# Turning normalized tokens into channels on VectorE in 32x32 blocks where no convolution runs

## The chip, the core and the metric

The kernel runs on one core of a Trainium2 chip. A core has five engines that work side by side, each through its own queue in order: TensorE (PE, matrix multiplication, with its weight loads shown apart as PEld), VectorE (DVE), ScalarE (ACT), GpSimd (POOL) and SyncE (SP), which here only issues DMA transfers. TensorE writes to PSUM, a small memory of eight banks; everything else lives in SBUF, with 128 partitions. The metric is device microseconds for one execution, fewer being better.

## The reference

The input is a batch of 2 images of 56 x 56 tokens with 384 channels, in fp32. Layer 0 is neighborhood attention with 12 heads of 32 channels over a 7 x 7 window, and a feed-forward network (MLP). Layer 1 is a depthwise 3 x 3 convolution with four scans over rows and columns, and a second MLP. Each step adds its input to its output.

```python
# layer 0
h = neighborhood_attention(layer_norm(x, ln1_g, ln1_b), w_qkv, b_qkv, rpb, w_proj, b_proj)
x = x + h
y = layer_norm(x, ln2_g, ln2_b)
x = x + gelu(y @ w1 + b1) @ w2 + b2
# layer 1
p = _layernorm(x, n1_g, n1_b) @ w_in + b_in
local = conv3x3_depthwise(p, k_conv)
mixed = 0.25 * (ema(local, left) + ema(local, right) + ema(local, down) + ema(local, up)) + local
x = x + _layernorm(mixed, on_g, on_b) @ w_out + b_out
h2 = _layernorm(x, n2_g, n2_b)
x = x + gelu(h2 @ w1 + b1) @ w2 + b2
```

Every layer norm works on a token's 384 (or 768) channels, and every product contracts over channels.

## The kernel before

The kernel computes in fp32 throughout. The work falls into three stages.

**Attention** runs over 14 groups of 448 tokens (8 rows of an image), each cut into 4 windows of 8 x 14 queries, each window into 3 units of 4 heads. One step `s` of the loop at L702 is one unit; there are 168. A unit's scores (L515) go to two PSUM banks, `biased` (L530, DVE) adds the bias, `numerators` (L536, ACT) takes the exponential into `pts`. The keys of a window lie in `m` chunks, two at the images' edges and three inside. `gathered` (L538) adds the chunks up on VectorE into `sum`, one step later. `values` (L546), two steps later, multiplies `pts` by the values `vt`, chunk by chunk, and then `sum` by ones (L558), which gives the denominators. Between these, TensorE computes queries, keys and values of later groups and projects finished tiles of 128 tokens (`project`, L573). In the last two groups (`n >= END`) there is nothing left to prepare beyond the last group's own queries, and projections come at the fixed steps in `THEN`. A projected tile is added to its residual `xr` (L585) after GpSimd has added a bias to `xr` (L571), either some steps after its load (`loaded`, a countdown from 4, L797) or just before the addition. The store of the tile is issued by `store_all` at the start of the next step, and right behind it the load of the residual of the tile three further on, into the buffer that the store reads (`bufs=3`). SP's queue is in order: these loads, the windows' `vt` (L465), the biases (L316) and, from step 152 on, the first MLP's six weight parts of 0.8 MB (L620) stand behind one another. At s == NU (L736) the keys' memory is given back, and the four last residuals and the first two groups of the attention's output (`xs`) are loaded. After the loop come the last projections, and the norm of `xs[0]` (L810). The PSUM banks of attention are then given back to the next stage, which needs their last readers, the additions at L585, to be done.

**The first pass** (L1341) runs over 13 groups of 2, 3 and then eleven times 4 tiles of 128 tokens. For a group `g` it computes twelve pieces of the hidden layer (`hidden`, L1053: a product from channels `hT`, then Gelu on ACT), and then the group's tokens, one tile at a time (`tokens`, L1059), in two PSUM banks called `y`. Beside this it takes the group before (`gw`, called `waiting`) on to layer 1: ACT normalizes it during hidden steps 2 to 5, `channels_n1` makes it into channels at step 11, and `project_in` multiplies by `w_in` and stores to `p_d`. The next group's norm (ln2) is taken during steps 3 to 10, and its `channels` stand after `project_in`, ahead of the tokens.

`channels` (L1038) calls `to_channels` (L245): for each of 3 channel blocks TensorE transposes each 128x128 piece (L251) into a PSUM bank, and ACT takes the bank to `hT` with the norm's gain and bias (L254).

**The convolution** runs on VectorE beside the two passes. A planner, `Beside` (L113), holds a list of jobs (`Band`, `Columns`), written out as small steps with an estimated cost. Each call `beside.go(worth)` in the passes lets out as many steps as are due. Jobs are added by `project_in` once enough image rows are there, for the first time while g is 3. `beside.busy()` tells whether any are left.

**The last pass** (L1428) runs over groups of eleven times 4, 3 and 2 tiles. The mixed tokens of a group are loaded by `load_mix` (L1233) two groups ahead as 6 channel blocks `mx`. Their norm's statistics are needed by token, so `measure` (L1246) transposes six 128x128 pieces per tile on TensorE (L1251) into PSUM, where VectorE reads them; `measure_beside` spreads the tiles over the hidden steps of the group before. `project_out` (L1266) multiplies by `w_out`. Then come the tokens of the group, and between its last two tiles the `channels` (n2) of the next. Group 6 is called `half_way`: its tokens reach into the second image, so the planner must be run to its end (`beside.until`) before `load_mix(6)`, at the end of g=4. For this group alone `measure_beside` starts two steps later (`late=2`).

Of the kernel before, what the change touches and what calls it, by code (L numbers as in the profile page):

```python
# [33 lines left out]
F32 = mybir.dt.float32  # L34
# [7 lines left out]
NH, KS, HD = 12, 7, 32  # L42
# [131 lines left out]
def block_kernel(ctx: ExitStack, tc: tile.TileContext, ins: dict, out: bass.AP):  # L174
# [328 lines left out]
    class Unit:  # L503
# [34 lines left out]
        def gathered(self):  # L538

            n, t = self.w.keys, lp.tile([P, 4, TT], F32, name="sum", bufs=2)  # L540
            self.sum = t
            nc.vector.tensor_tensor(t[:n], self.pts[:n, :, 0, :], self.pts[:n, :, 1, :], ALU.add)
            for c in range(2, self.m):
                nc.vector.tensor_tensor(t[:n], t[:n], self.pts[:n, :, c, :], ALU.add)

        def values(self):  # L546

            w, hg, n = self.w, self.hg, self.w.keys
            for c in range(self.m):
                for i in range(4):  # L550
                    h = 4 * hg + i
                    nc.tensor.matmul(
                        o[i * HD : (i + 1) * HD, hg, :],
                        lhsT=w.vt[:n, c, h * HD : (h + 1) * HD], rhs=self.pts[:n, i, c, :],
                        start=c == 0, stop=c == self.m - 1,
                    )
            for i in range(4):
                nc.tensor.matmul(  # L558
                    sums[i * HD : (i + 1) * HD, hg * TT : (hg + 1) * TT], lhsT=ones_hd[:n, :],
                    rhs=self.sum[:n, i, :], start=True, stop=True,  # L560
                )

    def load_residual(t, pool=lp, bufs=3):

        xrs[t] = pool.tile([P, C], F32, name="xr", bufs=bufs)
        nc.sync.dma_start(out=xrs[t], in_=xf[t * P : (t + 1) * P, :])
        loaded[t] = 4
# [134 lines left out]
    for s in range(NU + 4):  # L702
        n, k, hg, i = s // UG, s % UG, s % NC, s // NC
        store_all()
# [31 lines left out]
        if s == NU:  # L736
            kctx.close()
            xp = ctx.enter_context(tc.tile_pool(name="x", bufs=2, side="right", reuse_waits="tile"))
            tail_pool = actx.enter_context(tc.tile_pool(name="a_tail", bufs=1))
            for t in range(T2 // P - 4, T2 // P):  # L740
                load_residual(t, tail_pool, 4)
            xs = {g: load_group(x1f, groups[g], "xa") for g in range(2)}

# [63 lines left out]

    for take in taking:
        take()
    norm = norm_of(xs[0], groups[0][1], sm)  # L810
    norm.close(groups[0][1])
# [148 lines left out]
    def passes(xs, xn, w1, w2, between=lambda psum: None):  # L960
# [81 lines left out]

        def columns(w, m, hT, n):

            ps = ps_m.tile([P, MT], F32, name="mm")
            for c in range(NC):
                nc.tensor.matmul(  # L1047
                    ps[:, : n * P], lhsT=w[:, c, m * P : (m + 1) * P], rhs=hT[:, c, : n * P],
                    start=c == 0, stop=c == NC - 1,
                )  # L1050
            return ps
# [181 lines left out]
        def load_mix(g):  # L1233
            t0, n = dgroups[g]
            mx = io.tile([P, NI, MT], F32, name="mx")
            for b, at, here, n in images(t0, n * P):
                nc.sync.dma_start(
                    out=mx[:, :, here : here + n],
                    in_=mix_d[b][:, :, at : at + n].rearrange("m p t -> p m t"),
                )  # L1240
# [16 lines left out]
        def measure_beside(m, g, ahead, late=0):  # L1257

            n = dgroups[g][1]
            k = (m - late) // 2 - 1  # L1260
            if m % 2 == 1 and 0 <= k < n:
                measure(ahead[0], ahead[2], k)
            if m == min(10 + late, NHID - 1):
                ahead[2].close(n)
# [73 lines left out]
        def channels_n1(xn, n):  # L1338
            return channels(xn, n, "L1_conv_n1_g", "L1_conv_n1_b")

        for g, (t0, n) in enumerate(groups):  # L1341
            hid = []
            preparing = prepare_w_out() if g == 1 else iter(())
# [4 lines left out]
            for m in range(NHID):  # L1348
                next(preparing, None)
                if waiting is not None:  # L1350
# [5 lines left out]
                    if 2 <= m < 2 + groups[gw][1]:  # L1356
                        norm_w.apply_by_scalar(m - 2, x2w, xn_w)
                    if m == (11 if g == 1 else 6):
                        store_x2(gw, x2w)
                    if m == NHID - 1:  # L1360
                        hT_w = channels_n1(xn_w, groups[gw][1])
# [27 lines left out]
            if g < last:  # L1389
                hT = channels(xn_next, n_next, "L0_conv_ln2_g", "L0_conv_ln2_b")  # L1390
# [23 lines left out]
        hT = channels_n1(xn, groups[g][1])  # L1414
# [12 lines left out]
        hT = channels(first["xn"], dgroups[0][1], "L1_conv_n2_g", "L1_conv_n2_b")  # L1427
        for g, (t0, n) in enumerate(dgroups):  # L1428
            hid = []
            for m in range(NHID):  # L1430
                hid.append(hidden(w1, m, hT, n, "L1_conv_b1"))
                if g < last:
                    measure_beside(m, g + 1, ahead, 2 if g + 1 == half_way else 0)
# [6 lines left out]
            for k in range(n):  # L1440
                if k == n - 1 and g < last:
                    hT = channels(xn, dgroups[g + 1][1], "L1_conv_n2_g", "L1_conv_n2_b")
                ps = tokens(hid, w2, k)
                o = res[:, k, :]
                if k == 0 and g < last:
                    norm.shift(dgroups[g + 1][1])
                nc.vector.tensor_tensor(o, ps, o, ALU.add)  # L1447
                nc.sync.dma_start(out=yout[t0 + k * P : t0 + (k + 1) * P, :], in_=o)
                if k == n - 3 and g < last:
                    xn = normalized(norm, x3, dgroups[g + 1][1])  # L1450
# [95 lines left out]
```

## Time and profile before

| | us |
|---|---|
| median of 3 runs | 2710.99 (2710.21 to 2712.02) |
| the profiled execution, its own time | 2709.48 |
| its span, first to last instruction | 2707.7 |

The main groups of instructions of the profile, by line, as far as the change touches them or their neighbours (busy time is that of the group taken together, so pipelined instructions count once):

| line, engine | what | count | busy us | mean ns |
|---|---|---|---|---|
| L1063 PE | tokens, `y<-w,hid` | 2352 | 764.8 | 486 |
| L1047 PE | hidden, `mm<-hT,w` | 1872 | 776.1 | 570 |
| L251 PE | transposes of `channels`, 128x128 | 441 | 55.4 | 275 |
| L1251 PE | transposes of `measure`, 128x128 | 294 | 40.8 | 276 |
| L254 ACT | `hT<-tp`, 128x512 form | 99 | 69.7 | 776 |
| L482, L498 DVE | block transposes in attention, 128x352 | 56 + 56 | 30.5 + 30.0 | 544, 536 |
| L558 PE | sums, in all its forms | 1344 | 63.1 | 259 to 261 |
| L1141 DVE | taps of the convolution | 336 | 377.1 | 1122 |

How to read the profile: each engine has a row of 40 slices, and a digit is its busy share in tenths. Durations of matmuls are from start to modelled end and overlap, so what one costs in a stream is the distance between starts. A wait is named after the engine and line that released it. One fp32 matmul appears as two instructions, one transpose as one. The granted clock (PEclk) is TensorE's clock as a share of full speed.

### The profile page before, as it was taken

To read this page: it belongs to the slowest core of one execution; us is meant where nothing else is said; L and a number is where in the kernel's file an instruction comes from. 1 tells how busy PE (TensorE), PEld (TensorE's weight loads), DVE (VectorE), ACT (ScalarE), POOL (GpSimd) and SP (SyncE) were. 2 spreads that over 40 slices of the span, in tenths; PEclk is the share of its full clock that TensorE was granted. 3 is DMA by queue.
4 is the path that set the end of the run, shared out by engine and by line. 5 is a ranking of instruction groups with operands and counts; after the bars stand their busy time and mean duration, and the time that the engine had idled before them with its cause. 6 is when DMAs were issued, how large, how long until landed. Compare 5 with 4: busy or idle time off the path is not lost. (4 is left out here: it accounts for less than half of the span.)

```text
span 2707.7 us, 36333 instructions
## 1 busy us (share of the span) xinstructions
PE 2659.7 (98%) x14975; PEld 1492.9 (55%) x14975; DVE 1679.7 (62%) x2560; ACT 897.7 (33%) x1447; POOL 249.6 (9%) x264
## 2 busy tenths in 40 slices
PE   8999999998899999999999999999999999999998
PEld 4666666655555555555554555555555455555565
DVE  3778877878320188688989888898888522221110
ACT  4555555554222332222344422321233211111111
POOL 1111111111211100000010000000100011110100
PEclk9999999999999999999999999999999999999999
DMA  6423454225410132232354544443354411011000
GB/s 213 133 88 104 150 174 149 77 75 167 135 47 27 64 115 79 104 118 98 120 199 183 206 143 141 164 136 117 142 188 171 153 47 44 12 41 35 30 12 16
DMA packets 131887, 298.91 MB, mean 110 GB/s; under 512 B 10646, under 2 KB 87552, under 8 KB 129408
## 3 DMA queue, kind: packets, MB, share of 16 engines
q1 hardware_dynamic: 131712, 296.50, 31.9%
q8 instruction: 119, 1.95, 0.3%
q14 instruction: 56, 0.46, 0.1%
HBM read 180.86 MB, written 115.61 MB: 109 GB/s over the span
## 5 line engine op out<-in xcount | busy, mean ns | idle before, releaser
L1047 PE MATMUL mm<-hT,w 128*128 128x512 f32 (+2 forms) x1872 | 776.1, 570 | 0.1
L1063 PE MATMUL y<-w,hid 128*128 128x384 f32 x2352 | 764.8, 486 | 0.0
L1063 PEld LDWEIGHTS y<-w,hid 128*128 128x128 f32 x2352 | 445.0, 190 | 305.3 <-issue 0.5
L1047 PEld LDWEIGHTS mm<-hT,w 128*128 128x128 f32 x1872 | 352.1, 191 | 372.8 <-issue 342.4
L1056 ACT ACTIVATE hid<-mm,chan 128x512 f32<-128x512 f32 (+2 forms) x312 | 206.3, 662 | 741.2 <-PE mm L1047 741.2
L1141 DVE SCALAR_TENSOR_TENSOR loc<-pt,taps,loc 128x990 f32<-128x990 f32 (+9 forms) x336 | 377.1, 1122 | 10.0 <-ACT loc L1123 1.7
L536 ACT ACTIVATE pts<-pts 119x448 f32<-119x448 f32 (+3 forms) x336 | 206.5, 642 | 187.9 <-DVE pts L530 187.9
L530 DVE TENSOR_TENSOR pts<-sc,bias 119x448 f32<-119x448 f32 (+3 forms) x336 | 220.8, 699 | 67.7 <-PE sc L515 66.7
L222 POOL TENSOR_TENSOR rs<-rs,mhalf 128x4 f32<-128x4 f32 (+4 forms) x67 | 87.2, 1302 | 1745.6 <-DVE rs L219 1704.1
L386 PE MATMUL ps<-hT,wqkv 128*128 128x448 f32 x504 | 211.9, 559 | 3.5 <-ACT vs L431 1.5
L1047 PE MATMUL mm<-hT,w_in 128*128 128x512 f32 (+2 forms) x468 | 191.7, 568 | 0.6 <-ACT hT L254 0.6
L1063 PE MATMUL y<-w_out,mx 128*128 128x384 f32 x588 | 191.8, 486 | 0.0
L1395 DVE TENSOR_TENSOR xc<-y,xa 128x384 f32<-128x384 f32 x49 | 27.3, 557 | 251.0 <-PE y L1063 250.5
L1447 DVE TENSOR_TENSOR xc<-y,xc 128x384 f32<-128x384 f32 x49 | 27.2, 555 | 218.2 <-PE y L1063 167.8
L1063 PEld LDWEIGHTS y<-w_out,mx 128*128 128x128 f32 x588 | 111.6, 190 | 79.8 <-issue 4.8
L240 ACT ACTIVATE xn<-xc,sh,rs 128x384 f32<-128x384 f32 x98 | 64.7, 698 | 269.3 <-DVE sh L233 269.1
L214 DVE BATCH_NORM_STATS2 st<-xi 128x6 f32<-128x384 f32 x98 | 50.3, 554 | 153.3 <-PE xi L1251 153.2
L1047 PEld LDWEIGHTS mm<-hT,w_in 128*128 128x128 f32 x468 | 88.7, 190 | 101.6 <-issue 91.8
L386 PEld LDWEIGHTS ps<-hT,wqkv 128*128 128x128 f32 x504 | 90.2, 191 | 84.4 <-issue 72.8
L254 ACT ACTIVATE hT<-tp,chan 128x512 f32<-128x512 f32 (+2 forms) x117 | 79.5, 751 | 165.1 <-PE tp L251 165.0
L515 PEld LDWEIGHTS sc<-qT,kT 32*100 32x100 f32 (+3 forms) x3168 | 90.9, 169 | 69.5 <-DVE pts L530 17.3
L515 PE MATMUL sc<-qT,kT 32*100 32x112 f32 (+3 forms) x3168 | 113.8, 270 | 9.0 <-DVE pts L530 8.4
(89 smaller groups left out, 2435.4 us busy)
## 6 DMA issues: line engine op xcount, KB each, us to landing
bias<-in_bias_t SPq DMA_DIRECT2D x16, 1344.0 KB
loc<-loc_d SPq DMA_DIRECT2D x24, 784.0 KB
mixed<-mix_d SPq DMA_DIRECT2D x24, 784.0 KB
mix_d<-mixed SPq DMA_DIRECT2D x24, 784.0 KB
xa<-x_d SPq DMA_DIRECT2D x22, 768.0 KB
p_d<-mx SPq DMA_DIRECT2D x10, 1536.0 KB
mx<-mix_d SPq DMA_DIRECT2D x10, 1536.0 KB
pt<-p_d SPq DMA_DIRECT2D x18, 560.0 KB
```

The costliest lines, as they stand in the source:

```text
L214: nc.vector.bn_stats(st[:n, i, :], x)
L222: nc.gpsimd.tensor_tensor(rs, rs, mhalf[:n, :k], ALU.pow)
L240: nc.scalar.activation(out[:, k, :], x[:, k, :], AF.Identity, bias=self.sh[:n, k : k + 1], scale=self.rs[:n, k : k + 1],)
L254: nc.scalar.activation(dst[:, c, : len(xs) * n], tp, AF.Identity, bias=col(b, c), scale=col(g, c))
L386: nc.tensor.matmul(ps, lhsT=wqkv[:, c, m * P : (m + 1) * P], rhs=hT[:, c, half_of(n)], start=c == 0, stop=c == NC - 1,)
L515: nc.tensor.matmul(sc[i // 2][: w.keys, i % 2, (first + c) * TT : (first + c + 1) * TT], lhsT=kT[d, hg, w.keys_at + r * w.kc : w.keys_at + ...
L530: nc.vector.tensor_tensor(self.of(half), sc[half][:n, :, at].rearrange("p h (c q) -> p h c q", q=TT), self.w.bias[:n, 4 * self.hg + h : 4 ...
L536: nc.scalar.activation(self.of(half), self.of(half), AF.Exp)
L1047: nc.tensor.matmul(ps[:, : n * P], lhsT=w[:, c, m * P : (m + 1) * P], rhs=hT[:, c, : n * P], start=c == 0, stop=c == NC - 1,)
L1056: nc.scalar.activation(t[:, : n * P], ps[:, : n * P], AF.Gelu, bias=col(b1, m))
L1063: nc.tensor.matmul(ps, lhsT=t[:, k * P : (k + 1) * P], rhs=w[:, m, :], start=m == 0, stop=m == len(lhs) - 1,)
L1141: nc.vector.scalar_tensor_tensor(to, pt[:, lo + dy - self.top : hi + dy - self.top, xt : xt + n], self.tap(dy, dx), to, ALU.mult, ALU.add,)
```

## The change

Where no convolution runs, the transposition of normalized tokens into channels goes from TensorE to VectorE. This engine turns 32x32 blocks; so a 128x128 piece is turned by 16 instructions, one for each pair of 32-partition strips, each over all channel blocks at once. In both passes the flag `by_vector` decides, and in the last pass `measure_by_vector` replaces `measure` for the groups after half way. Three other parts go with it: in attention's last two groups the denominators are summed over the chunks by TensorE instead of VectorE; the loads at s == NU move to the start of the step, with `xs` ahead of the residuals, and the norm of `xs[0]` ahead of the takes; the load of the half-way group is cut by tiles, and its `late` goes.

```diff
         def gathered(self):
-            n, t = self.w.keys, lp.tile([P, 4, TT], F32, name="sum", bufs=2)
-            self.sum = t
+            n, self.parts = self.w.keys, [self.pts[:, :, c, :] for c in range(self.m)]
+            if self.w.n >= END:
+                return
+            t = lp.tile([P, 4, TT], F32, name="sum", bufs=2)
+            self.parts = [t]
...
-            for i in range(4):
-                nc.tensor.matmul(
-                    sums[i * HD : (i + 1) * HD, hg * TT : (hg + 1) * TT], lhsT=ones_hd[:n, :],
-                    rhs=self.sum[:n, i, :], start=True, stop=True,
-                )
+            for c, part in enumerate(self.parts):
+                for i in range(4):
+                    nc.tensor.matmul(
+                        sums[i * HD : (i + 1) * HD, hg * TT : (hg + 1) * TT], lhsT=ones_hd[:n, :],
+                        rhs=part[:n, i, :], start=c == 0, stop=c == len(self.parts) - 1,
+                    )
...
-        loaded[t] = 4
+        loaded[t] = steps
...
     for s in range(NU + 4):
         n, k, hg, i = s // UG, s % UG, s % NC, s // NC
+        if s == NU:
+            kctx.close()
+            xp = ctx.enter_context(tc.tile_pool(name="x", bufs=2, side="right", reuse_waits="tile"))
+            tail_pool = actx.enter_context(tc.tile_pool(name="a_tail", bufs=1))
+            xs = {g: load_group(x1f, groups[g], "xa") for g in range(2)}
+            for t in range(T2 // P - 4, T2 // P):
+                load_residual(t, tail_pool, 4, 2)
         store_all()
...
-        if s == NU:
-            kctx.close()
...
-            for t in range(T2 // P - 4, T2 // P):
-                load_residual(t, tail_pool, 4)
-            xs = {g: load_group(x1f, groups[g], "xa") for g in range(2)}
...
+    norm = norm_of(xs[0], groups[0][1], sm)
+    norm.close(groups[0][1])
     for take in taking:
         take()
-    norm = norm_of(xs[0], groups[0][1], sm)
-    norm.close(groups[0][1])
...
+        def turned(xn, k, hT):
+            for i in range(0, P, HD):
+                for j in range(0, P, HD):
+                    nc.vector.transpose(
+                        hT[j : j + HD, :, k * P + i : k * P + i + HD],
+                        xn[i : i + HD, k, :].rearrange("p (c q) -> p c q", c=NC)[:, :, j : j + HD],
+                    )
+
+        def scaled(hT, n, g, b):
+            for c in range(NC):
+                nc.scalar.activation(
+                    hT[:, c, : n * P], hT[:, c, : n * P], AF.Identity, bias=col(b, c),
+                    scale=col(g, c),
+                )
...
+            step = P if g == half_way else n * P
+            for t in range(0, n * P, step):
+                for b, at, here, size in images(t0 + t, step):
+                    here += t
+                    nc.sync.dma_start(
+                        out=mx[:, :, here : here + size],
+                        in_=mix_d[b][:, :, at : at + size].rearrange("m p t -> p m t"),
+                    )
...
+        def measure_by_vector(mx, norm, k):
+            t = flat(half("turned", "work"))[:, : NI * P]
+            for i in range(0, P, HD):
+                for j in range(0, P, HD):
+                    nc.vector.transpose(
+                        t[j : j + HD].rearrange("p (m c) -> p m c", m=NI)[:, :, i : i + HD],
+                        mx[i : i + HD, :, k * P + j : k * P + j + HD],
+                    )
+            norm.add(k, [t[:, h * C : (h + 1) * C] for h in range(2)])
+
+        def measure_beside(m, g, ahead):
             n = dgroups[g][1]
-            k = (m - late) // 2 - 1
-            if m % 2 == 1 and 0 <= k < n:
-                measure(ahead[0], ahead[2], k)
-            if m == min(10 + late, NHID - 1):
+            if g > half_way:
+                if m % 2 == 0 and m // 2 < n:
+                    measure_by_vector(ahead[0], ahead[2], m // 2)
+            elif m % 2 == 1 and 0 < m // 2 <= n:
+                measure(ahead[0], ahead[2], m // 2 - 1)
+            if m == 10:
                 ahead[2].close(n)
...
         for g, (t0, n) in enumerate(groups):
             hid = []
+            by_vector = 0 < g < last and not beside.busy()
...
+                    if by_vector and m == 2:
+                        hT_w = io.tile([P, NC, MT], F32, name="hT")
+                    if by_vector and 3 <= m < 3 + groups[gw][1]:
+                        turned(xn_w, m - 3, hT_w)
...
-                    if m == NHID - 1:
-                        hT_w = channels_n1(xn_w, groups[gw][1])
+                    if m == NHID - 1 and by_vector:
+                        scaled(hT_w, groups[gw][1], *n1)
+                    elif m == NHID - 1:
+                        hT_w = channels(xn_w, groups[gw][1], *n1)
...
-            if g < last:
-                hT = channels(xn_next, n_next, "L0_conv_ln2_g", "L0_conv_ln2_b")
+            if by_vector:
+                hT = io.tile([P, NC, MT], F32, name="hT")
+                for k in range(n_next):
+                    turned(xn_next, k, hT)
+                scaled(hT, n_next, *ln2)
+            elif g < last:
+                hT = channels(xn_next, n_next, *ln2)
...
         for g, (t0, n) in enumerate(dgroups):
+            by_vector = half_way <= g < last
...
-                    measure_beside(m, g + 1, ahead, 2 if g + 1 == half_way else 0)
+                    measure_beside(m, g + 1, ahead)
...
             for k in range(n):
-                if k == n - 1 and g < last:
-                    hT = channels(xn, dgroups[g + 1][1], "L1_conv_n2_g", "L1_conv_n2_b")
+                if by_vector and 0 < k < n - 1:
+                    for q in range(2 * k - 2, min(2 * k, dgroups[g + 1][1])):
+                        turned(xn, q, hT)
+                elif by_vector and k == n - 1:
+                    scaled(hT, dgroups[g + 1][1], *n2)
+                elif k == n - 1 and g < last:
+                    hT = channels(xn, dgroups[g + 1][1], *n2)
                 ps = tokens(hid, w2, k)
...
+                if k == 0 and by_vector:
+                    xn = normalized(norm, x3, dgroups[g + 1][1])
+                    hT = io.tile([P, NC, MT], F32, name="hT")
...
                 if k == n - 3 and g < last:
-                    xn = normalized(norm, x3, dgroups[g + 1][1])
+                    if not by_vector:
+                        xn = normalized(norm, x3, dgroups[g + 1][1])
                     add_row(x3, dgroups[g + 1][1], "b2_1")
```

## The prediction

> **What bounds the kernel now.** I read the page's rows of busy time first, then the slices, then the waits of TensorE alone, then windows.
>
> ```profile
> PE 2659.7 (98%) x14975; PEld 1492.9 (55%) x14975; DVE 1679.7 (62%) x2560; ACT 897.7 (33%) x1447; POOL 249.6 (9%) x264
> ...
> PE   8999999998899999999999999999999999999998
> ...
> DVE  3778877878320188688989888898888522221110
> ```
> TensorE (PE) works throughout; VectorE (DVE) is nearly empty in two places, slices 13 to 15 and from slice 33 on. These are groups 1 to 3 of the first pass and the second half of the last pass, where no convolution runs. Next, TensorE's own waits, longest first:
>
> ```profile
> PE sc L515 <- DVE pts L530: 8.4, 15, 1.5
> PE tp L251 <- DVE bad L820: 7.4, 1, 7.4
> PE ps L357 <- DVE xg L226: 7.3, 1, 7.3
> PE xi L1251 <- DMA mx<-mix_d: 4.8, 1, 4.8
> PE o L552 <- DMA vt<-v_d: 3.4, 5, 1.0
> PE sums L558 <- DVE sum L542: 3.3, 4, 1.2
> ```
> Little else is lost: the end of attention (`sc`, `vt`, `sums`, `tp`) and one wait for the mixed tokens at half way (`xi`). Windows of these places (first two: attention's last two groups; then its end, half way, one group of the last pass):
>
> ```profile
> 610.30:652.40 42.10, 38.79 (x650) 24.29 (x648) 34.72 (x70) 19.88 (x35) 2.86 (x8) 1.00 0.40 136
> 652.40:687.00 34.60, 25.75 (x512) 16.98 (x512) 29.61 (x66) 14.37 (x29) 7.58 (x13) 1.00 0.67 211
> 687.00:708.20 21.20, 13.82 (x46) 7.92 (x43) 8.33 (x21) 1.31 (x2) 7.14 (x9) 0.88 0.62 199
> ...
> 2134.00:2144.00 10.00, 5.32 (x13) 2.09 (x11) 0.00 (x0) 2.06 (x3) 0.00 (x0) 0.99 1.04 336
> 2211.50:2292.80 81.30, 81.30 (x254) 44.76 (x253) 16.33 (x31) 12.86 (x19) 8.85 (x4) 1.00 0.12 39
> ```
> Columns: length, busy PE, weight loads, DVE, ACT, POOL, granted clock, DMA share, GB/s. In the last window PE has no gap and DVE works 16 of 81 us. There, whatever leaves PE's queue leaves the span, as long as DVE delivers.
>
> **1. Transposes that leave TensorE.** Their price, from the timeline of PE:
>
> ```profile
> 2221.78 0.82 PE L1251 MATMUL xi<-ident,mx 128*128 128x128 f32 x6
> 2222.43 5.32 PE L1047 MATMUL mm<-hT,w 128*128 128x512 f32 x12
> ```
> Six transposes push the next matmul from 2221.78 to 2222.43: 0.65 us, 0.109 each (twelve `tp` take 1.31). Count, in 128-token tiles:
> - n1 in g=1..3 (`gw` 0, 1, 2): 2+3+4 = 9 tiles; ln2 for groups 2, 3, 4: 12 tiles. `beside` gets its first jobs inside g=3, after `by_vector` was taken; from g=4 it has planned work of some 120 us against 82 us spent by g=5, and more comes each group. So 21 tiles x 3 = 63.
> - n2 for groups 7..12 of the last pass: 4+4+4+4+3+2 = 21 tiles x 3 = 63.
> - `measure` for the same groups: 21 x 6 = 126.
>
> 252 x 0.109 = **27.5 us** off PE. ACT still writes three pieces per group, so nothing moves there.
>
> **2. What VectorE takes on.** 16 block transposes per tile: 32x96 (`turned`) or 32x192 (`measure_by_vector`). Nearest row: `STREAM_TRANSPOSE` of 128x352, 536 to 544 ns. With the smallest DVE rows at 182 ns (6 elements) the slope is about 1.04 ns an element, so 32x96 is about 0.27 and 32x192 about 0.37 us. That is a duration; two independent `bn_stats` of 555 ns took 1.03 us together, so neighbours overlap by some 0.08. By that row: 0.19 and 0.29. Against it stands the Trainium skill, "VectorE: DVE Perf Modes", section "Two Vector instructions with no wait between them": an instruction whose input or output starts in another 32-partition quadrant than the one before is held until all earlier ones have finished. Here `j` changes the output's quadrant every time, so all would be held. No row of before has such neighbours. Held, with the 0.03 us seen between dependent instructions, I take 0.31 and 0.41. By the row a group of four tiles costs DVE 12 + 19 us, by the rule 20 + 26; ends: 0.19 and, if size counts for nothing, 0.54.
>
> Are they late at the rule's price? Last pass, g=6..9. Tokens start at 2179.2; the first add ends at 2187.7; then come 64 transposes and one add: 2187.7 + 19.8 + 0.6 = 2208.1, then `scaled`, 0.7 for the first third. The next hidden layer is due at 2211.47 - 1.31 = 2210.2. It fits; break-even is (2210.2 - 2187.7 - 0.6 - 0.7)/64 = 0.33 us. The adds queued behind (k=1, 2) have 7.7 us, a second `y` bank. The measures start with the hidden layer: 4 x (16 x 0.41 + 1.3 of statistics) = 31.5 us; `rs` is wanted at about 33.6, and PE itself stalls only if the first `x3` is missing when the third tile begins, from about 0.48 us each. g=1..3: n1 takes 10 to 20 us, spread over hidden steps 3 to 11 (15 to 21 us); ln2 takes 20, with the adds of `x2` queued behind, hidden by project_in (7.7 to 15.5) and two tiles of tokens (15.4). Cost **0**, if the cover holds.
>
> **3. Sums in attention's last two groups.** 18 units lose one DVE add (0.62), 6 units two: 18.6 us off DVE. PE gets 30 more sets of eight matmuls (each matmul is two instructions); streaming, `o` does 24 in 0.54 us, so 0.18 a set, 5.4 us. Not all of it counts. In units 147 to 152 DVE is full, but PE is full beside it whenever a query or projection is there: gain 1 to 2. From 642 us the SP queue sets the pace: each `xr` load waits until the store of the tile three earlier has landed, behind a 0.8 MB weight part, and the next window's `vt` stands behind it:
>
> ```profile
> SPq L566 <- DMA x_d<-xr: 34.9, 7, 8.6
> ```
> A faster unit there only waits longer for `vt`. Ends -3 (PE-bound) and +8 (DVE alone binding); I take **+1.5**, near the SP row.
>
> **4. End of attention.** Now SP issues at s=168: store of tile 41 (688.36), `xr` 44 (693.33, after that store), four tail `xr`, `xa` (695.6). `xa` lands at 701.15, POOL's `rs` waits for it, four `xr` adds of 0.96 wait behind `rs`, and PE gets its banks at 708.2. After: `xa` and the tail loads go out from 688.4 and the tail adds ahead of `rs`. But the store of 41 and `xr` 44 come last: at the 0.28 MB per us that a window from 689 to 693 shows, 0.8 MB of weights, 1.0 of `xa`, 0.8 of `xr` and the store are through at about 699.6, `xr` 44 lands 2.5 later at 702, POOL adds it by 703.2, DVE by 703.8. `norm_of` ahead of the takes puts the adds of tiles 42 and 43 behind `xa` (about 696.2), so tile 46 starts 2 us late; tile 48's wait covers that. Tile 48 needs the bank of 44: PE 703.9 to 705.9, first transpose about 706.7. Gain **1.5**, between 0 and 6 if DMA is faster; the granted clock, 0.50 from 703.3 to 713.6 now, may give back up to 2.5 more, which I leave to the range.
>
> **5. Half way.** `late` goes: PE wants tile 0 after four hidden layers instead of six, at 2134.2 rather than 2139.3. The load is cut by tile, five DMAs instead of two, so PE waits for 64+64 tokens only. They still stand behind the last store of the mix; 768 packets of 256 B took 1.1 us, so two such are down at about 2141 (the whole landed at 2144.0). Wait 6.9 instead of 4.8: **-2.1**. The later tiles come in time. Ends -5 (clock half speed for longer) and +2.
>
> Sum: 27.5 + 0 + 1.5 + 1.5 - 2.1 = **28.4 us**. The profiled execution took 2709.48 (span 2707.7), 1.5 under the median 2710.99 of the runs; from the median: **2682.5 us**.
>
> **Rivals.**
> - *VectorE delivers late.* Between 0.33 and 0.43 us per 32x96 block, hidden layers of g=6..9 wait: at 0.40, 4 x 64 x 0.07 = 18 us, total 2700. For it: nothing measured so small. Against: the row's slope.
> - *It is slower than before.* Same place, four waits per last pass. It decides from 0.33 + 28.4/256 = 0.44 us. If each block costs 0.54 like the 128x352 row: 4 x 64 x 0.21 = 54 us, total 2736. For it: the skill's "VectorE: DVE Perf Modes", "Rules for kernel authors", gives 128x128 transposes to TensorE. Against: 6-element rows at 182 ns; size counts.
> - *Attention's end pays.* If DVE, not SP, held groups 12 and 13 (34.7 of 42.1 and 29.6 of 34.6 us busy), and the gap at 700.8 closes with the clock kept: 8 + 8 instead of 3, total 2669.
> - *`beside` is busy sooner*, so the first pass keeps its 63 transposes: 6.9 less, 2689.5.
>
> **Numbers.** Forecast 0.58, attention pays 0.18, late but still faster 0.12, first pass unchanged 0.05, slower than before 0.05, lost in small waits 0.02. Range 2668 to 2699: from the attention rival to the late blocks. A measurement here tells 0.2% (5.4 us) from no change: faster 0.91, within 0.04, slower 0.05.
>
> **What would show it.** Step 1: `tp` falls from 441 to 315 and `xi` from 294 to 168, and a four-tile group of the last pass from 81.3 to 77.4 us. Step 2: mean and pitch of the new transposes; no PE wait on `hT` or on `y`'s banks in g=6..11. Step 3: `vt` waits up, `sums` waits gone. Step 4: first transpose after attention near 707, PE waiting once on an `xr` add. Step 5: one PE wait for `mx` near 7 us. The forecast is wrong if PE waits for `hT` at each group of the last pass, or if attention ends over 5 us earlier.

## The result, and the profile after

The changed kernel takes **2684.57 us** (median of 4 runs, 2681.68 to 2685.53), against 2711.15 before (4 runs on the same chip): 26.6 us less, ratio 0.990 with an interval of 0.9885 to 0.9915. The profiled execution took 2684.19, its span 2682.4 (before: 2709.48 and 2707.7). The forecast was 2682.5 with 28.4 us less.

The rows of busy time and the slices, as shown of before:

```profile
PE 2641.6 (98%) x14963; PEld 1474.9 (55%) x14963; DVE 1963.1 (73%) x3538; ACT 898.9 (34%) x1447; POOL 250.3 (9%) x264
...
PE   8999999999899999999999999999999999999998
...
DVE  3778877876365688688989888888888627677652
```

TensorE lost 18 us of busy time and VectorE won 283. The two places where VectorE was nearly empty are slices 12 to 14 (the prediction miscounts them as 13 to 15) and those from 33 on; 12 to 14 and 34 to 39 now stand at 5 to 7 tenths. TensorE is as full as before; it just has less to do. Its own waits, longest first (engine, what and where it waited for; sum in us, times, longest):

```profile
PE xi L1276 <- DMA mx<-mix_d: 7.3, 1, 7.3
PE ps L357 <- DVE xg L226: 7.3, 1, 7.3
PE sc L515 <- DVE pts L530: 5.5, 10, 1.3
PE o L556 <- DMA vt<-v_d: 5.1, 5, 1.8
PE sums L563 <- DVE sum L546: 1.2, 1, 1.2
PE ps L582 <- DVE xr L590: 1.1, 1, 1.1
...
PE tp L251 <- DVE bad L825: 0.7, 1, 0.7
```

The wait for `mx` has grown from 4.8 to 7.3 and that for `vt` from 3.4 to 5.1; the 7.4 us in front of the first transpose after attention have shrunk to 0.7. There is no wait on `hT` in the last pass. Windows, in the order of those of before (attention's group 12, its group 13, its end, the wait half way, the hidden layers behind that wait, one group of four tiles of the last pass; columns: length, busy PE, weight loads, DVE, ACT, POOL, granted clock, DMA share, GB/s):

```profile
610.30:652.40 42.10, 41.26 (x782) 27.43 (x784) 24.56 (x51) 20.05 (x35) 2.85 (x8) 1.00 0.40 133
653.40:691.70 38.30, 31.04 (x616) 22.26 (x616) 23.41 (x53) 14.44 (x29) 7.54 (x13) 0.89 0.63 196
691.70:708.70 17.00, 15.12 (x47) 8.39 (x44) 7.22 (x21) 1.31 (x2) 7.13 (x9) 0.94 0.72 244
2125.80:2133.10 7.30, 0.01 (x1) 0.02 (x1) 0.00 (x0) 0.69 (x1) 0.00 (x0) 0.84 1.09 279
2133.10:2137.50 4.40, 4.38 (x10) 2.66 (x11) 1.34 (x3) 0.00 (x0) 0.00 (x0) 0.50 1.15 324
2206.30:2283.60 77.30, 77.30 (x217) 41.04 (x216) 56.53 (x159) 12.98 (x19) 8.87 (x4) 1.00 0.12 41
```

The last row is the change at its best: the group takes 77.3 us instead of 81.3, TensorE still has no gap, and VectorE works 56.5 us of it instead of 16.3.

To see where the time went, I set the same TensorE instruction of both traces side by side. The difference of their start times, after less before:

| at | after less before, us |
|---|---|
| first transpose after attention | +0.5 |
| first tokens of the first pass | -1.7 |
| end of the first pass's groups 1 to 3 | -8.4 |
| whole stretch with convolutions beside it (953 to 2115) | -8.4 |
| first hidden layers after half way | -5.2 |
| end of the last pass | -25.9 |

So 6.6 us come from the first pass (8.4 less 1.7) and 20.7 from the last (25.9 less 5.2), and 3.2 are lost half way (8.4 less 5.2). Attention as a whole comes out about even (+0.5), with 2.2 got back just behind it, where the clock returns to full speed earlier (693.7 instead of 713.6). The spans differ by 25.3; I did not place the remaining 0.6.

### The profile page after: what moved, and what is told of

It reads as the page before. It is cut to its first block, busy times and chain, and to the rows that moved or that the text cites. A ratio compares the mean times of both kernels' runs of the same rounds, so it can differ in the third digit from the quotient of the medians.

```text
span 2682.4 us, 37273 instructions
## 1 busy us (share of the span) xinstructions
PE 2641.6 (98%) x14963; PEld 1474.9 (55%) x14963; DVE 1963.1 (73%) x3538; ACT 898.9 (34%) x1447; POOL 250.3 (9%) x264
## 4 chain that ended last, share of the span: by engine, by line
PE 72%; ACT 0%; DVE 0%; DMA 0%; issue 0%; ACTq 0%
PE y L1084 35%; PE mm L1068 35%; PE tp L251 1%; PE xi L1276 1%; ACT line L1209 0%; DMA mx<-mix_d 0%; PE y L1020 0%; DVE line L1113 0%; DMA mix_d<-mixed 0%; DVE mixed L1236 0%; PE ps L582 0%; ACT hT L254 0%; ACT xn L240 0%; ACT hid L1077 0%; DVE line L1109 0%
## 5 line engine op out<-in xcount | busy, mean ns | idle before, releaser
L530 DVE TENSOR_TENSOR pts<-sc,bias 119x448 f32<-119x448 f32 (+3 forms) x336 | 220.8, 699 | 76.5 <-PE sc L515 74.2
L1052 DVE STREAM_TRANSPOSE hT<-xn 32x96 f32<-32x96 f32 x672 | 181.1, 269 | 31.3 <-PE mm L1068 11.7
L1287 DVE STREAM_TRANSPOSE turned<-mx 32x192 f32<-32x192 f32 x336 | 123.3, 367 | 4.2
L556 PE MATMUL o<-pts,vt 100*32 100x112 f32 (+3 forms) x3168 | 112.8, 267 | 6.1 <-DMA vt<-v_d 5.1
```

The source lines that it names most:

```text
L530: nc.vector.tensor_tensor(self.of(half), sc[half][:n, :, at].rearrange("p h (c q) -> p h c q", q=TT), self.w.bias[:n, 4 * self.hg + h : 4 ...
L556: nc.tensor.matmul(o[i * HD : (i + 1) * HD, hg, :], lhsT=w.vt[:n, c, h * HD : (h + 1) * HD], rhs=self.pts[:n, i, c, :], start=c == 0, stop ...
L1052: nc.vector.transpose(hT[j : j + HD, :, k * P + i : k * P + i + HD], xn[i : i + HD, k, :].rearrange("p (c q) -> p c q", c=NC)[:, :, j : j ...
L1287: nc.vector.transpose(t[j : j + HD].rearrange("p (m c) -> p m c", m=NI)[:, :, i : i + HD], mx[i : i + HD, :, k * P + j : k * P + j + HD],)
```

## The experiments

All are edits of the changed kernel (below, `-` is the changed kernel's line, `+` the experiment's). Times are medians; "before" is the kernel before in the same series of runs: 2711.56 us for the first four, 2709.71 for the next four, 2709.55 for the last three. The changed kernel was timed beside another 2711.15. So where an experiment is set against the changed kernel, I compare what each takes off its own "before"; for the changed kernel that is 26.6 us.

For attention I use three stretches of the profiled execution: from the first bias addition (L530) of group 12 to that of group 13, from there to the first of the last seven projections, from there to the first transpose. In us:

| kernel | group 12 | group 13 | end | sum |
|---|---|---|---|---|
| before | 42.1 | 34.6 | 21.2 | 97.9 |
| after | 43.3 | 38.3 | 16.9 | 98.5 |
| no turns | 43.3 | 36.6 | 20.2 | 100.1 |
| half way loaded whole | 43.3 | 39.3 | 16.9 | 99.5 |
| sums on VectorE | 42.1 | 39.0 | 15.4 | 96.5 |
| old order at the end | 43.3 | 36.5 | 21.1 | 100.9 |
| each transpose twice | 43.3 | 35.6 | 18.6 | 97.5 |
| neighbours in one strip | 43.3 | 37.9 | 18.8 | 100.0 |
| four residual buffers | 43.3 | 33.0 | 14.6 | 90.9 |
| half way measured later | 43.3 | 38.6 | 19.8 | 101.7 |
| both | 43.3 | 31.4 | 14.6 | 89.3 |
| both, sums on VectorE | 42.1 | 39.0 | 14.6 | 95.7 |
| both, sums on TensorE for group 13 only | 42.1 | 32.8 | 14.6 | 89.5 |

Six of these (after, no turns, half way loaded whole, twice, one strip, half way later) run the same attention, and their sums go from 97.5 to 101.7. Their group 13 goes from 35.6 to 39.3 and their end from 16.9 to 20.2; the clock is at half for 3.4 to 10.2 us of that group 13. A difference of two or three us in these columns is therefore no finding; group 12, which repeats to 0.1, and the fall of the sum to about 90 are.

**No turns.** All transposes back to TensorE; the rest of the change stays.

```diff
-            if g > half_way:
+            if False:
...
-            by_vector = 0 < g < last and not beside.busy()
+            by_vector = False
...
-            by_vector = half_way <= g < last
+            by_vector = False
```

> The changed kernel with all transposes back on TensorE (by_vector off in both passes, measure for every group); the other parts stay. Theory (the 252 transposes carry the whole gain, 27.5 us; attention's end gains 1.6 and half way loses 3.2): 2712.5 us, 1.5 slower than before, ratio near 1.0006. Rival (the new order at attention's end or the sums pay for a part): 2706 or less, ratio below 0.998.

Measured: 2712.52 (13 runs), ratio to before 1.0005 [0.9997, 1.0014]. Without the moved transposes nothing of the gain is left: they are the gain, and the other parts together are worth between a gain of 0.8 us and a loss of 3.8.

**Half way loaded whole.** The old load in one piece, measured two steps later.

```diff
-            step = P if g == half_way else n * P
...
+            for b, at, here, n in images(t0, n * P):
...
-            elif m % 2 == 1 and 0 < m // 2 <= n:
-                measure(ahead[0], ahead[2], m // 2 - 1)
-            if m == 10:
+            elif m % 2 == 1 and 0 <= (m - (2 if g == half_way else 0)) // 2 - 1 < n:
+                measure(ahead[0], ahead[2], (m - (2 if g == half_way else 0)) // 2 - 1)
+            if m == (11 if g == half_way else 10):
```

> The changed kernel with the half-way group loaded whole and measured two steps later, as before. Theory (measuring two steps earlier costs more wait than the cut load saves, 3.2 us by the traces): 2681.4 us, and TensorE's wait for mx back at 4.8 us. Rival (the load is late however it is cut, so nothing is lost): 2684.6 us, wait of 7 us.

Measured: 2680.79, ratio 0.9888 [0.9873, 0.9903], and TensorE's wait for `mx` is 4.8 us again:

```profile
PE xi L1272 <- DMA mx<-mix_d: 4.8, 1, 4.8
```

The cut load with the earlier measure costs 2.5 us of wait. By the medians it costs 4.2 (30.8 off "before" against 26.6), but the intervals of the two kernels overlap; the trace's 2.5 and what the clock adds behind it is the firmer figure.

**Sums on VectorE.** The early return is taken out, so groups 12 and 13 add their parts on VectorE as before.

```diff
             n, self.parts = self.w.keys, [self.pts[:, :, c, :] for c in range(self.m)]
-            if self.w.n >= END:
-                return
```

> The changed kernel with the sums of attention's last two groups back on VectorE. Theory A (the SP queue sets the pace there): within 1.5 us of 2684.6. Theory B (TensorE is the bound in group 12, its 30 added sets of sums cost): 2 to 4 us faster, 2681 to 2682.5. Theory C (VectorE was the bound, the change freed it): 5 us or more slower, over 2689.

Measured: 2682.16, ratio 0.9896 [0.9881, 0.9911], an interval that overlaps the changed kernel's. Group 12 takes 42.1 us instead of 43.3, as before: the extra sums on TensorE cost it 1.2. In group 13 the sums make no difference that can be told (39.0 against 38.3). So here this part of the change gives nothing and takes about one us, by the trace.

**Old order at the end of attention.** Residuals first, then `xa`, both at the end of step `s == NU`, all four steps of every projection, the norm after the takes.

```diff
-        if s == NU:
...
-            xs = {g: load_group(x1f, groups[g], "xa") for g in range(2)}
-            for t in range(T2 // P - 4, T2 // P):
-                load_residual(t, tail_pool, 4, 2)
         store_all()
...
+        if s == NU:
...
+            for t in range(T2 // P - 4, T2 // P):
+                load_residual(t, tail_pool, 4)
+            xs = {g: load_group(x1f, groups[g], "xa") for g in range(2)}
...
-    norm = norm_of(xs[0], groups[0][1], sm)
-    norm.close(groups[0][1])
     for take in taking:
         take()
+    norm = norm_of(xs[0], groups[0][1], sm)
+    norm.close(groups[0][1])
```

> The changed kernel with the loads at s == NU back behind store_all, residuals first with the countdown of 4, and the norm of xs[0] behind the takes. Theory (by the traces the stretch from the first of the last seven projections to the first transpose shrank from 21.2 to 17.1 us): 4 us slower, 2688.5 us, and TensorE's one wait ahead of the transposes back at 7 us. Rival (the residual of tile 44 sets the end in either order): within 1.5 us of 2684.6.

Measured: 2689.86 (5 runs), ratio 0.992 [0.9906, 0.9933]: some 5 us slower than the changed kernel by the medians (21.7 off "before" against 26.6), though the intervals just overlap. The wait in front of the first transpose is back and the end takes 21.1 us, as before:

```profile
PE tp L251 <- DVE bad L825: 7.2, 1, 7.2
```

With it the clock is at half from 706.6 to 716.8, into the first pass; in the changed kernel it was back at full at 693.7. So the new order takes this wait away; how many of the 5 us are the wait's and how many the clock's is not shown, and the sum of the three stretches (100.9) lies within the spread of kernels that have the new order.

**Each transpose twice.** In the last pass every block transpose of the normalized tokens is issued twice in a row, with the same data.

```diff
+                    for _ in range(times):
                         nc.vector.transpose(
...
-                        turned(xn, q, hT)
+                        turned(xn, q, hT, 2)
```

> The changed kernel with each 32x96 block transpose of the last pass (n2, groups 7 to 12) issued twice in a row; the first pass and the measures stay. Theory (nothing is paid until VectorE's chain passes the 0.33 us per block of the prediction; two transposes at a pitch of 0.283 make 0.566): TensorE waits for hT at the start of the hidden layers, 64 x (0.566 - 0.33) = 15 us for each of four groups and some 5 and 3 for the two short ones, in all about 65 us: 2750 us. Rival (VectorE has slack to spare, as 73% busy says): under 2690. If the second of each pair, writing the same strip, is not held and costs 0.19, the pair is 0.47: 9 us for each of four groups, about 2722.

Measured, in its one run: 2772.15 us. TensorE's waits from 2150 us on:

```profile
PE mm L1069 <- ACT hT L1060: 43.4, 6, 10.1
PE y L1085 <- DVE xc L1509: 22.2, 5, 4.4
```

VectorE around one of them (start, length, line, operation, tiles; the last number is how many run in a row):

```profile
2269.76 9.38 DVE L1053 STREAM_TRANSPOSE hT<-xn 32x96 f32<-32x96 f32 x32
2279.17 0.56 DVE L1509 TENSOR_TENSOR xc<-y,xc 128x384 f32<-128x384 f32 x1
2279.64 18.77 DVE L1053 STREAM_TRANSPOSE hT<-xn 32x96 f32<-32x96 f32 x64
2298.44 1.02 DVE L1509 TENSOR_TENSOR xc<-y,xc 128x384 f32<-128x384 f32 x2
```

The cover that the prediction named is gone, and the waits are where its signs of being wrong put them: at each hidden layer, since `hT` comes too late, and at the second bank of `y`, whose `xc` add stands behind the transposes. Their sum is 65.6 us where some 65 were expected, although the expectation had named `hT` alone. Of a pair, the second transpose writes what the first wrote and waits for it, so it starts 0.034 us after the first has ended; a pair takes 0.587 us (18.77 by 32) where 0.566 was expected. The whole came out 22 us above the expected 2750, and the clock fits that: after 2150 it is at half for 72 us in eleven stretches, in the changed kernel for 8 in one. About 41 of the 72 lie under matmuls; at half the speed they are, by my estimate, 20 us of delay. A wait for VectorE is paid here once as a wait and again in the matmuls behind it.

**Neighbours in one strip.** The loop over tiles goes innermost, so that two block transposes in a row read and write the same strips of 32 partitions.

```diff
             for i in range(0, P, HD):
                 for j in range(0, P, HD):
+                  for k in ks:
...
-                    for q in range(2 * k - 2, min(2 * k, dgroups[g + 1][1])):
-                        turned(xn, q, hT)
+                    turned(xn, range(2 * k - 2, min(2 * k, dgroups[g + 1][1])), hT)
```

> The changed kernel with the loops of turned reordered where several tiles are turned together (ln2 in the first pass, n2 in the last): the tile is the innermost loop, so that two to four neighbours read and write the same strips. If instructions are held only by a change of strip: the first of each set starts about 0.28 us after the one before, the others some 0.19 to 0.20 us. If every block transpose runs to its end before the next: all at 0.28. The time stays in both cases within 1.5 us of 2684.6, since TensorE waits for none of them.

Measured: 2685.72, ratio 0.9905 [0.9889, 0.9922], no change from the changed kernel that can be told. Groups by shape (busy us, mean ns of one), the changed kernel and then this one:

```profile
L1052 DVE STREAM_TRANSPOSE hT<-xn 32x96 f32<-32x96 f32 x672 | 181.1, 269 | 31.3 <-PE mm L1068 11.7 <-ACT xn L240 10.9
L1287 DVE STREAM_TRANSPOSE turned<-mx 32x192 f32<-32x192 f32 x336 | 123.3, 367 | 4.2
```

```profile
L1053 DVE STREAM_TRANSPOSE hT<-xn 32x96 f32<-32x96 f32 x672 | 147.8, 250 | 27.4 <-PE mm L1069 11.7 <-ACT xn L240 10.9
```

The same 672 transposes occupy VectorE for 33 us less. In the last pass the second of a pair starts 0.20 us after the first, the first of the next pair, with another strip, 0.24 after that (in the first pass's sets of four the third and fourth start after 0.16 each); in the changed kernel every one starts 0.283 after the one before. The kernel doesn't gain from it: VectorE was in time already.

**Four residual buffers.** The rival to "VectorE holds attention's end" is SP's queue, where a residual load waits for a store and the `vt` loads stand behind it. A fourth buffer takes that wait away.

```diff
-    def load_residual(t, pool=lp, bufs=3, steps=4):
+    def load_residual(t, pool=lp, bufs=4, steps=4):
```

> The changed kernel with four buffers for the residuals of attention instead of three, so that the load of the tile three further on no longer waits for the store of the tile just finished. Theory (the SP queue stands still behind that wait, and vt and the last residual behind it): TensorE's waits for vt, 5.1 us, go, and the wait for the last residual too; with the clock held, 5 to 8 us faster, 2677 to 2680. Rival (the transfers themselves fill the time, 195 GB/s in group 13): within 2 us of 2684.6.

Measured: 2676.31, ratio 0.9877 [0.9861, 0.9894]: 33.4 us off "before" against 26.6, so 6.8 more than the changed kernel, though the intervals just overlap. The longest wait of SP's queue between 640 and 705 us, changed kernel and then this one:

```profile
SPq L571 <- DMA x_d<-xr: 37.5, 7, 8.7
```

```profile
SPq L609 <- DVE xc L1446: 31.9, 1, 31.9
```

The residual's wait for a store has gone from the queue; what is left longest is the load of `xa` for a later group of the first pass, which waits until that pass gives a buffer free. TensorE no longer waits for `vt`:

```profile
PE xi L1276 <- DMA mx<-mix_d: 7.3, 1, 7.3
PE ps L357 <- DVE xg L226: 7.1, 1, 7.1
PE sc L515 <- DVE pts L530: 6.8, 11, 1.3
PE sums L563 <- DVE sum L546: 1.2, 1, 1.2
```

The rival in the expectation, that the transfers themselves fill the time, is out: in group 13 the core moves 243 GB/s here, 196 in the changed kernel.

**Half way measured later.** The load stays cut, but the four tiles are measured after hidden layers 7 to 10, and the norm closes at 11.

```diff
+            elif g == half_way:
+                if 7 <= m < 7 + n:
+                    measure(ahead[0], ahead[2], m - 7)
             elif m % 2 == 1 and 0 < m // 2 <= n:
                 measure(ahead[0], ahead[2], m // 2 - 1)
-            if m == 10:
+            if m == (11 if g == half_way else 10):
```

> The changed kernel with the cut load of the half-way group kept, and its four tiles measured on TensorE after hidden steps 7 to 10 instead of 3, 5, 7, 9, closed at 11. Theory (the 7.3 us wait and the half clock after it, some 2.2 us, exist only because the tiles are asked for too early): no wait for mx, 9 us faster, 2675.5 us. Rival (the wait moves on to project_out, which then lacks rs): under 4 us faster, over 2680.

Measured: 2674.41, ratio 0.9866 [0.9849, 0.9882]: 35.3 us off "before", 8.7 more than the changed kernel, and the intervals are apart. The same window, half way, of the changed kernel and then of this one:

```profile
2100.00:2160.00 60.00, 52.69 (x158) 27.61 (x157) 28.14 (x36) 10.36 (x15) 4.46 (x2) 0.94 0.52 169
```

```profile
2100.00:2160.00 60.00, 60.00 (x187) 32.20 (x186) 31.06 (x41) 13.02 (x19) 4.45 (x2) 1.00 0.52 169
```

TensorE works all 60 us at full clock. The core moves the same 169 GB/s in both; the tiles are just not wanted so early. The 7.3 us of wait were a choice of order, not of the load. Whether the load has to be cut for this was not tried.

**Both**, then the sums once more. The two last edits together; then the same with the sums back on VectorE; then with the sums on TensorE only for group 13.

```diff
-            if self.w.n >= END:
+            if self.w.n > END:
                 return
```

> The changed kernel with four residual buffers in attention and the half-way tiles measured after steps 7 to 10. Theory (the two gains lie in different places and add, 8.3 + 10.2 us): 2666 us, no wait of TensorE for vt or mx. Rival (they share something, for instance the clock): 2670 or more.

> As the kernel with both (four residual buffers, half-way tiles after steps 7 to 10), with the sums of attention's last two groups on VectorE. Theory (group 12 is TensorE's, 42.1 us with the sums on VectorE and 43.3 without; once SP no longer holds group 13, VectorE does): group 12 gains 1.2 and group 13, 33.0 us with the sums on TensorE, goes back to 36 or more: 2 to 3 us slower than with both, 2668 to 2669. Rival (the sums belong on VectorE in both groups): 1 to 3 us faster than with both.

> As the kernel with both (four residual buffers, half-way tiles after steps 7 to 10), with the sums of group 12 on VectorE and those of group 13 alone on TensorE. Theory (each group's sums on the engine that has room): 1.2 us faster than with both, 2665 us. Rival (nothing left there): the same within 1 us.

Measured: both, 2667.48, ratio 0.9844 [0.9831, 0.9858]; with the sums on VectorE 2670.63, 0.9857 [0.9842, 0.9872]; with the sums on TensorE for group 13 alone 2667.84, 0.984 [0.9827, 0.9854]. TensorE's longest waits in "both":

```profile
PE ps L357 <- DVE xg L226: 7.1, 1, 7.1
PE sc L515 <- DVE pts L530: 5.4, 9, 1.3
PE sums L563 <- DVE sum L546: 1.2, 1, 1.2
```

Neither `mx` nor `vt` is left among the long ones. "Both" takes 42.1 us off the kernel before, 15.5 more than the changed kernel; that is the sum of 6.8 and 8.7, so the two gains add, as expected.

What the sums do is seen in the traces. Group 12 takes 43.3 us with its sums on TensorE and 42.1 with them on VectorE: there they cost 1.2 whatever the queue does. Group 13 in "both" and then with the sums on VectorE (columns as above), and TensorE's longest wait in the second:

```profile
652.90:684.30 31.40, 27.61 (x616) 19.99 (x616) 22.54 (x53) 14.26 (x29) 7.60 (x13) 1.00 0.79 247
651.00:689.90 38.90, 30.47 (x512) 20.13 (x512) 29.59 (x66) 14.46 (x29) 7.57 (x13) 0.87 0.65 204
...
PE sums L561 <- DVE sum L544: 4.6, 5, 1.2
```

TensorE's gaps, length less busy time, tell the two causes apart. With the sums on VectorE they are 8.5 us with three residual buffers and 8.4 with four: the free queue gives nothing, since TensorE then waits for VectorE. With the sums on TensorE and three buffers they are 5.3 to 8.4 in the six executions, with waits for `vt`. With the sums on TensorE and four buffers they are 3.8. The queue and VectorE each hide the other, and it takes both parts to gain.

The 7.6 us between the two stretches are not all VectorE's, though. In the second the clock is at half for 10.2 us, which is up to 5.1 us of delay, and the kernel before, with its sums on VectorE and the clock at full, took 34.6. So 2.5 to 3.2 us are what the sums' place is worth at a like clock, by this estimate. The total shows about as much: 3.2 us between "both" and the same with the sums on VectorE, whose intervals overlap, though no run of the one reaches a run of the other (2664.92 to 2668.40, and 2670.34 to 2671.67). The 1.2 us expected from sums on TensorE for group 13 alone cannot be told: its median lies 0.4 above that of "both", and its runs go from 2663.68 to 2669.68.

## Why the prediction was right, point by point

**Step 1, transposes off TensorE: right.** Forecast 27.5 us, 6.9 in the first pass and 20.6 in the last; measured 6.6 and 20.7. The count held (`tp` 315, `xi` 168), and so did the price of 0.109 us taken from the start of the next matmul. The kernel with no turns shows that this is all of the gain. Priced by their durations, 273 and 278 ns, the 252 would have been 69 us.

```profile
L251 PE MATMUL tp<-ident,xn 128*128 128x128 f32 x315 | 39.0, 273 | 0.7 <-DVE bad L825 0.7
L1276 PE MATMUL xi<-ident,mx 128*128 128x128 f32 x168 | 23.6, 278 | 7.3 <-DMA mx<-mix_d 7.3
```

**Step 2, VectorE at no cost: right, and for the reason given.** The durations that the slope gave, 0.27 and 0.37, came out at 0.269 and 0.367. Between the row and the rule I took the rule of the Trainium skill ("VectorE: DVE Perf Modes", "Two Vector instructions with no wait between them"), and the trace agrees with it: each transpose starts 0.013 us after the one before has ended, 0.283 from start to start (0.383 for the wide ones), and the neighbours in one strip overlap, at 0.20. (Those of "each transpose twice" lie in one strip too and do not overlap, but there the second waits for the first; the rule is for instructions with no wait between them.) The forecast of 0.31 and 0.41 had 0.03 of pause where 0.013 was measured. VectorE in one turn of the last pass, changed kernel:

```profile
2261.09 9.03 DVE L1052 STREAM_TRANSPOSE hT<-xn 32x96 f32<-32x96 f32 x32
2270.16 0.56 DVE L1508 TENSOR_TENSOR xc<-y,xc 128x384 f32<-128x384 f32 x1
2270.63 9.03 DVE L1052 STREAM_TRANSPOSE hT<-xn 32x96 f32<-32x96 f32 x32
2279.70 0.56 DVE L1508 TENSOR_TENSOR xc<-y,xc 128x384 f32<-128x384 f32 x1
```

ScalarE begins with `scaled` at 2279.70 and its first third is through by about 2280.4; the next hidden layer starts at 2283.64. That leaves 3.2 us for 64 transposes, 0.05 each: the break-even is at 0.283 + 0.05 = 0.33 us, as forecast. Twice the transposes shows that the cliff is real; one point beyond it, with 65.6 us of waits where about 65 were expected from 0.33, fits this place for it but does not pin it down.

**Step 3, sums: wrong in sign.** "I take +1.5, near the SP row" was the step. For group 12 it said "gain 1 to 2", and the relief was of that size: TensorE's gaps there fell by 1.8 us, from 3.3 to 1.5. But its busy time rose by 3.0, from 38.8 to 41.8, since nearly every set of sums put on it is paid, and the group lost 1.2. The kernel with the sums back on VectorE shows it. For group 13 "SP sets the pace" was right once the sums had moved: the waits for `vt` grew, those on `sums` went from four to one, and the fourth buffer took the `vt` waits away. In the kernel before, though, VectorE held this group as well, as the fourth buffer with the sums on VectorE shows: it gives nothing there. The stretch took 38.3 us instead of 34.6, with the clock at half for 8.3 of them, up to 4.1 us of delay; the step had no term for that.

**Step 4, end of attention: right in kind.** Forecast 1.5, measured 4.3 in the stretch (21.2 to 16.9). The six executions with this attention have 16.9 to 20.2 there, so the gain is 1.0 to 4.3 and the forecast lies inside. TensorE waits once on an `xr` add, 1.1 us, as said. The first transpose came at 708.7, where 706.7 was forecast, since groups 12 and 13 had given away 4.9 us beforehand. The clock, for which the range allowed up to 2.5 us to be got back, did come back earlier, and 2.2 us were got back behind the first transpose.

**Step 5, half way: the direction right, the size 1.1 too small.** Forecast -2.1, measured -3.2. The wait was 7.3 instead of 6.9, and the clock behind it was left to the range ("clock half speed for longer"), not put into the sum: it is at half for the 4.4 us of hidden layers shown above, which is 2.2 us of delay, against 1.5 before (work resumed at 2144.1, the clock was full from 2147.1). So 2.5 of the 3.2 are wait and 0.7 are clock.

The misses in the profiled executions: 0.2 in step 1, 6.4 in step 3 (a loss of 4.9 for a gain of 1.5), 1.1 in step 5; on the other side 2.8 in step 4 and 2.2 from the clock behind it. That makes 25.7 of 28.4, and the end of the last pass moved by 25.9. Steps 1 and 2 are what the forecast stands on, and they hold by their mechanism. That attention's misses nearly cancelled is in part luck.

## What to carry to other kernels

Where one engine is full and has no gaps, price work moved off it by how much later its next instruction starts, not by the duration of the work; and check the receiving engine not by its sum but at the one place where its result is due, with the break-even per instruction. A reordering that leaves a first-in-first-out load queue as it is moves waits about: the further gains here (7 and 9 us) came from one more buffer, so that a load waits for no store, and from using a late transfer later. Put work on the full engine only in those stretches where the other one sets the end: the same sums cost 1.2 us in one group and, with the load queue free, save about 3 in the next, more where the clock falls with the gaps. And where two causes hold a stretch, taking one away may show nothing.

## What was not expected of the hardware

**The clock needs no long gap to fall.** In the changed kernel it is at half from 656.2 to 659.6 and from 686.9 to 693.7. In the 11 us before the first fall TensorE has one gap over 0.25 us, of 1.34; before the second it has three, of 0.92, 0.89 and 1.83. The half-speed stretches of all the profiled executions last 3.4, 6.8 or 10.2 us, except the one at a run's end. The Trainium skill ("TensorE: Matmul & The Clock Gate", "Why this matters for your kernels") asks for no gaps over about 3 us; in this trace shorter ones went ahead of a fall. The length of a gap doesn't decide it alone: in "both" a gap of 1.34 us at 652.2 passes without a fall, and so do six gaps of 0.8 to 1.5 us in the kernel before, between 651 and 685. What decides stays open. The fastest of the changed kernel's four runs (2681.68) has a mean clock of 0.996, the other three 0.995.

**Small block transposes pay for changing strips**: 0.283 us from start to start where each output lies in another strip than the one before, 0.20 where it doesn't and no wait stands between the two, for the same 32x96 elements.
